# A postnorm layer on one core: the second batch's second low-rank factor later, the last norms partly on ScalarE, one queue for each half

## The chip, the cores and the metric

The kernel runs on one core of a Trainium2 chip. The metric is the time of one execution on the device in microseconds. Engines are called by the profile's names: PE (TensorE matmul), PEld (its weight load), DVE (VectorE), ACT (ScalarE), POOL (GpSimd), SP (SyncE). All data is f32.

## The reference

One transformer layer on `x` of 2 batches x 512 tokens x 512 features: grouped attention with 32 query heads and 8 key heads of size 128, then a feed-forward part with a mixture of four low-rank experts. After each part a residual is added and a layer norm without weights is applied.

```python
x = layernorm(x + attention(x) @ Wo + bo)                       # causal softmax, rotary embedding
y = x @ W_base.T + b_base                                       # 512 -> 512
z = x @ A[e].T                                                  # 4 experts, rank 8: 32 numbers a token
alpha = softmax(log(prior + eps) + (x @ router_W.T + router_b)) # over the 4 active experts
out = layernorm(x + y + sum_e alpha[e] * 2 * z[e] @ Bm[e].T)
```

## The kernel before, in words

Tokens are cut into eight tiles of 128: four (`TPB`) of the first batch, four of the second. Attention is a software pipeline over the tiles of all head groups, driven by `slot(T)`. At its end the feed-forward part starts, one object `Ffn` a tile. Nothing is rearranged by a scheduler: each engine executes its instructions in the order in which the Python code issues them, and the code after the last `slot` is an order written out by hand.

The steps of one `Ffn`, which the code calls as methods:

- `stats`, `centre`, `transpose`: the first norm (with `norm1.root` for the reciprocal root of the variance), and the tile transposed by PE.
- `base(c)`, c = 0 to 3: two matmuls for each quarter of the features, one into each of the tile's two PSUM banks `py[0]` and `py[1]`. Each bank holds 256 of the 512 outputs, and beside them half of `z`; the second holds the router's four logits too (L679). In the profile each matmul appears as two records, so that `base` of all four quarters is "x16".
- `logits`, `alphas`: DVE adds the prior and takes the maximum (L696, L698), ACT takes the exponential (L705), DVE normalises (L706, L707) and multiplies `z` by the weights into `zs` (L710).
- `low_rank`: PE transposes `zs` into the PSUM tile `tz` (L719), and DVE copies that to `zT` (L720). `tz` lies in the pool `ps_k`, which has one buffer, so that two tiles' `low_rank` share it.
- `finish`: the second low-rank factor, two matmuls of 33 rows that add onto `py` (L724, "x4").
- `add`: DVE adds the residual from both banks into `y` (L730) and takes the second norm's statistics (L634, L635).
- `norm2.root` (ACT square root L638, DVE reciprocal L639), then `store`: POOL subtracts the mean and multiplies (L642), SP's queue sends the tile out (L754).

The last tile is done differently. `route` computes its `z` and logits ahead by matmuls of 16 and 20 columns (L689). `half` and `half_end` compute 256 outputs at a time and add the residual and the low-rank part in PSUM (L738, L744, L745); `half_stats` takes the statistics from there (L748, L750); `store_halves` normalises each half out of PSUM (L642) and sends it (L760).

Names at the end: `fz` is the fourth tile of the first batch, `fa[0]` and `fa[1]` are the first two of the second batch in the order of work, `fb` and `fc` the last two. `fz` and `fb` use the banks `qx` and `qy`, `fa[0]` and `fc` the two `sc` banks, `fa[1]` the banks `wx` and `wy`.

The order written out by hand around the change, with the methods' names:

```python
fc.route(*CTX); fc.logits(); fc.alphas(); fa[1].logits(); fa[1].alphas()
fa[0].finish(); fa[0].add()
fa[1].low_rank()
# fb.base(0), fb.base(1), fa[1].finish(), fa[1].add(), fb.base(2), fb.base(3)
fc.low_rank()
# roots and stores of fz and fa; fb.logits, fb.alphas; first half of fc; fb.low_rank
# second half of fc with fb.finish and fb.add inside; fb's root and store; fc's
```

Of the kernel before, what the change touches and what calls it, by code (L numbers as in the profile page):

```python
# [9 lines left out]
F32 = mybir.dt.float32  # L10
I32 = mybir.dt.int32
AF = mybir.ActivationFunctionType
ALU = mybir.AluOpType
AX = mybir.AxisListType

P = 128
# [13 lines left out]
def postln_layer_kernel(  # L30
# [33 lines left out]
    nc = tc.nc  # L64
# [35 lines left out]
    outf = out.flatten_outer_dims()  # L100
# [17 lines left out]
    OH, ARH = O // 2, EAR // 2  # L118
# [54 lines left out]
    for n in range(2):  # L173
# [6 lines left out]
        out=tri, in_=tri, pattern=[[-BLK, QB], [-1, BLK]], compare_op=ALU.is_ge,  # L180
# [221 lines left out]
    halves = {}  # L402
# [221 lines left out]
    class Norm:  # L624
# [16 lines left out]
        def apply(self, i, dst, src=None, engine=nc.vector):  # L641
            engine.tensor_scalar(  # L642
                dst, dst if src is None else src, self.mv[:, i, 0:1], self.rstd[:, i : i + 1], ALU.subtract, ALU.mult)

    class Ffn:


# [101 lines left out]
            if n:  # L749
                nc.vector.bn_aggr(self.norm2.mv[:, self.i, :], self.st)  # L750

        def store(self):
            self.norm2.apply(self.i, self.y, engine=nc.gpsimd)
            nc.sync.dma_start(out=outf[ts(self.t, P), :], in_=self.y)  # L754

        def store_halves(self):
            for n, queue in enumerate((nc.sync, nc.scalar)):
                cols = ts(n, OH)
                self.norm2.apply(self.i, self.y[:, cols], self.py[n])
                queue.dma_start(out=outf[ts(self.t, P), cols], in_=self.y[:, cols])  # L760


    NP = len(parts)
# [209 lines left out]
    def tiles(ts_, banks, name):  # L973
        n = len(ts_)
        norms = Norm(ffn_pool, n, f"a{name}"), Norm(ffn_pool, n, f"f{name}")
        return [Ffn(t, bank, *norms, i) for i, (t, bank) in enumerate(zip(ts_, banks))]

    f0 = tiles(range(TPB), ((QX, QY), (QX, QY), (SC, SC), (QX, QY)), "0")
    fa = tiles([TPB + i for i in order[:2]], ((SC, SC), (WX, WY)), "1a")
# [75 lines left out]
    fa[1].alphas()  # L1055
    fa[0].finish()
    fa[0].add()
    fa[1].low_rank()
    for c in range(KC):
        fb.base(c)  # L1060
        if c == 1:
            fa[1].finish()
            fa[1].add()
    fc.low_rank()
    fz.norm2.root(3, TPB)
    fa[0].norm2.root(0, 2)
    for f in (fz, *fa):
# [12 lines left out]
            fb.add()  # L1080
    fc.half_end(1)
    fb.norm2.root(0, 1)
    fb.store()
    fc.half_stats(1)
    fc.norm2.root(0, 1)
    fc.store_halves()
# [50 lines left out]
```

## Time and profile before

| | |
|---|---|
| median of 3 runs | 840.73 us (840.07 to 843.15) |
| the profiled execution, its own time | 840.69 us |
| its span, first to last instruction | 838.9 us |
| PE busy | 826.0 us, 98% of the span |
| DVE, ACT, POOL busy | 595.7, 353.1, 292.3 us |
| mean granted PE clock | 0.996 |

The span is what the profile shows in detail; 1.8 us of the execution's own time lie around it. A row of the timeline gives start, duration, engine, line, operation, what it writes and reads, and in brackets the idle time of the engine before it with what ended that. The chain lists, from the end backwards, the work that each step had to wait for. The granted clock (PEclk) is 1.00 at full speed. Times below are microseconds from the start of the span, in the profiled execution.

### The profile page before, as it was taken

The page shows a single profiled execution, that of the slowest core. Times are in us where ns is not written, and L with a number is a line of the kernel's source. Part 1 is how long each engine was busy: PE and PEld are TensorE (multiplying, and loading weights), DVE is VectorE, ACT ScalarE, POOL GpSimd, SP SyncE. Part 2 cuts the span into 40 slices and gives each one's busy share as a digit, 9 for nine tenths or more (in the row PEclk, how much of TensorE's full clock was granted, in tenths as well). Part 3 has the DMA queues.
Part 4 walks back from the last instruction along what each step waited for, and adds up shares of the span by engine and source line. Part 5 has one row for each costly group of instructions (what it writes and reads, how often), then busy time and mean ns, then how long its engine had stood idle before and what let it go on. Part 6 is the DMA issues. An engine that isn't in the chain of part 4 may idle for free.

```text
span 838.9 us, 10734 instructions
## 1 busy us (share of the span) xinstructions
PE 826.0 (98%) x3201; PEld 583.9 (70%) x3201; DVE 595.7 (71%) x1963; ACT 353.1 (42%) x1000; POOL 292.3 (35%) x319
## 2 busy tenths in 40 slices
PE   9999999999999999999999999999999999999996
PEld 5567767677777777777777777777777776645564
DVE  5468977787767876786867867687767968853534
ACT  1225454544435344434435444434434444762132
POOL 6463344233332334233332334344323523300023
PEclk9999999999999999999999999999999999999998
DMA  9127536463653566362653566274644546574211
GB/s 287 40 64 195 151 97 183 110 181 108 156 157 99 164 162 174 77 188 88 154 149 104 163 159 182 69 217 116 153 129 133 164 110 191 165 236 113 62 39 63
DMA packets 84971, 116.47 MB, mean 139 GB/s; under 512 B 6581, under 2 KB 64797, under 8 KB 82866
## 3 DMA queue, kind: packets, MB, share of 16 engines
q1 hardware_dynamic: 84258, 115.50, 48.2%
q0 software_dynamic: 448, 0.14, 0.2%
q8 instruction: 25, 0.41, 0.2%
q14 instruction: 32, 0.26, 0.1%
q10 hardware_dynamic: 208, 0.15, 0.1%
HBM read 71.73 MB, written 44.04 MB: 138 GB/s over the span
## 4 chain that ended last, share of the span: by engine, by line
PE 92%; DVE 3%; DMA 1%; ACT 1%; POOL 1%; issue 1%; SPq 0%; DVEq 0%; POOLq 0%
PE pc L544 16%; PE sc L488 13%; PE qx L429 11%; PE wx L429 11%; PE pp L355 10%; PE qy L429 8%; PE wy L429 8%; PE pv L342 7%; PE py L679 3%; PE po L615 3%; PE tp L274 1%; PE py L724 1%; DMA x_sb<-_attn_hidden_states_dram 1%; DMA pT<-db 0%; DVE wt L568 0%
## 5 line engine op out<-in xcount | busy, mean ns | idle before, releaser
L503 ACT ACTIVATE p<-sc,nmax 128x288 f32<-128x288 f32 (+15 forms) x256 | 124.5, 486 | 253.0 <-DVE nmax L496 207.5
L496 DVE CUSTOM_DVE_ANT_0 sc<-sc,maskw 128x288 f32<-128x288 f32 (+15 forms) x256 | 114.2, 446 | 154.4 <-PE sc L488 151.7
L544 PE MATMUL pc<-pT,v 128*128 128x512 f32 x320 | 165.5, 599 | 0.5 <-DMA pT<-db 0.5
L488 PE MATMUL sc<-kT,qT 128*128 128x160 f32 (+15 forms) x512 | 162.0, 398 | 1.2 <-ACT p L503 1.1
L376 POOL TENSOR_TENSOR qT<-q,t 128x512 f32<-128x512 f32 x56 | 71.1, 1269 | 188.0 <-DVE q L375 188.0
L511 ACT ACTIVATE p<-p,den 128x288 f32<-128x288 f32 (+15 forms) x256 | 133.5, 522 | 0.1
L488 PEld LDWEIGHTS sc<-kT,qT 128*128 128x128 f32 x512 | 96.7, 190 | 30.3 <-issue 14.3
L416 POOL TENSOR_TENSOR cs<-ctxT 128x256 f32<-128x256 f32 x28 | 26.5, 947 | 196.1 <-PE wy L429 109.5
L550 ACT COPY ctxT<-pc 128x512 f32<-128x512 f32 x64 | 37.5, 586 | 124.0 <-PE pc L544 124.0
L519 DVE STREAM_TRANSPOSE zt<-p 128x128 f32<-128x128 f32 (+2 forms) x192 | 81.6, 425 | 0.0
L544 PEld LDWEIGHTS pc<-pT,v 128*128 128x128 f32 x320 | 57.0, 190 | 19.5 <-issue 5.7
L355 PE MATMUL pp<-xT,wk 128*128 128x512 f32 x128 | 65.0, 593 | 0.5 <-ACT xT L275 0.5
L342 PE MATMUL pv<-wv,xT 128*128 128x256 f32 x256 | 63.6, 379 | 0.0
L429 PE MATMUL wx<-wo,ctxT 128*128 128x256 f32 x224 | 57.7, 380 | 0.4 <-DVE den L507 0.4
L429 PE MATMUL qx<-xs,wq 128*128 128x256 f32 x224 | 58.0, 381 | 0.0
L342 PEld LDWEIGHTS pv<-wv,xT 128*128 128x128 f32 x256 | 48.5, 190 | 13.4 <-issue 6.9
L521 DVE STREAM_TRANSPOSE zt<-p 128x32 f32<-128x32 f32 (+3 forms) x256 | 57.4, 224 | 0.0
L429 PEld LDWEIGHTS qx<-xs,wq 128*128 128x128 f32 x224 | 41.4, 190 | 22.3 <-issue 16.0
L429 PEld LDWEIGHTS wx<-wo,ctxT 128*128 128x128 f32 x224 | 42.4, 190 | 13.5 <-issue 7.7
L503 ACT ACTIVATION_READ_ACCUMULATOR p<-sc,nmax 128x1 f32 x256 | 49.9, 195 | 0.0
L601 DVE TENSOR_TENSOR x_sb<-wx,x_sb 128x256 f32<-128x256 f32 x112 | 46.9, 419 | 0.0
L368 DVE SCALAR_TENSOR_TENSOR t<-q,bqkT,rope_sb 64x512 f32<-64x512 f32 x56 | 43.0, 768 | 1.3
(187 smaller groups left out, 1364.3 us busy)
## 6 DMA issues: line engine op xcount, KB each, us to landing
db<-zt SPq DMA_DIRECT2D x64, 256.0 KB, 4.3
pT<-db SPq DMA_DIRECT2D x16, 1024.0 KB, 4.8
db<-zt SPq DMA_DIRECT2D x64, 192.0 KB, 3.3
pT<-db SPq DMA_DIRECT2D x16, 768.0 KB, 4.4
wq<-in_L_attn_Wq_dram SPq DMA_DIRECT2D x20, 512.0 KB, 4.7
wo<-in_L_attn_Wo_dram SPq DMA_DIRECT2D x10, 1024.0 KB, 7.5
db<-zt SPq DMA_DIRECT2D x64, 128.0 KB, 2.4
pT<-db SPq DMA_DIRECT2D x16, 512.0 KB, 4.1
```

What stands on the lines that cost most here:

```text
L342: nc.tensor.matmul(psq["v", gg, t], lhsT=xT[:, c, ts(t, P)], rhs=wvs[gg][0][:, c, :], start=(c == 0), stop=(c == KC - 1))
L355: nc.tensor.matmul(psq[key], lhsT=wt[:, c, cols], rhs=xT[:, c, ts(b, S)], start=(c == 0), stop=(c == KC - 1))
L376: nc.gpsimd.tensor_tensor(dst, t1[:].rearrange("p (n s) -> p n s", s=BLK), t2[:].rearrange("p (n s) -> p n s", s=BLK), ALU.add)
L429: nc.tensor.matmul(ps, lhsT=wt[:, c, :], rhs=xt[:, c, :], start=start and c == 0, stop=c == CH - 1, skip_group_check=True)
L488: nc.tensor.matmul(sc[s][:, :w], lhsT=qT[u][:, i * QB + n].rearrange("p r s -> p (r s)"), rhs=kT[u][:].rearrange("p n s -> p (n s)")[:, :w ...
L496: nc.vector.tensor_tensor_reduce(sc[s][:, :w], sc[s][:, :w], maskw[:, S - w :], -SCALE, -MASKED, ALU.add, ALU.min, nmax[s])
L503: nc.scalar.activation(ptile[s][:, :w], sc[s][:, :w], AF.Exp, bias=nmax[s], scale=-1.0, accum_out=rden[s])
L511: nc.scalar.activation(ptile[s][:, :w], ptile[s][:, :w], AF.Copy, scale=rden[s])
L519: nc.vector.transpose(z[:, :, last - i : last, n, :].rearrange("p q j s -> p j q s"), ptile[s][:, : i * P])
L521: nc.vector.transpose(z[:, : n + 1, last, n, :], ptile[s][:, i * P : w])
L544: nc.tensor.matmul(psc[p], lhsT=v_sb[g // VG, b * TPB + j][:, ts(g % VG, D)], rhs=pT[p][:, :, ts(j, P)], start=(j == 0), stop=(j == i))
L601: nc.vector.tensor_tensor(into, pw[k, bank], into, ALU.add)
```

## The change

It does three things. `fa[1].low_rank` moves from before `fb.base(0)` to after `fb.base(2)`, and `fa[1].finish` and `fa[1].add` move from after `fb.base(1)` to after `fc.low_rank`. The second norm of `fb` is applied by ACT instead of POOL, as `rstd * y + shift` with a `shift = -mean * rstd` computed by one more DVE instruction; the first half of `fc` is treated in the same way, and its second half stays on DVE. The two halves of `fc` swap queues: the first goes out by ACT's queue, the second by SP's.

```diff
+        def apply_act(self, i, dst, src=None):
+
+            shift = self.pool.tile([P, 1], F32, tag="shift", name="shift", bufs=2)
+            mean, rstd = self.mv[:, i, 0:1], self.rstd[:, i : i + 1]
+            nc.vector.scalar_tensor_tensor(shift, mean, -1.0, rstd, ALU.mult, ALU.mult)
+            nc.scalar.activation(dst, dst if src is None else src, AF.Identity, bias=shift, scale=rstd)
...
-        def store(self):
-            self.norm2.apply(self.i, self.y, engine=nc.gpsimd)
+        def store(self, on_act=False):
+            if on_act:
+                self.norm2.apply_act(self.i, self.y)
+            else:
+                self.norm2.apply(self.i, self.y, engine=nc.gpsimd)
             nc.sync.dma_start(out=outf[ts(self.t, P), :], in_=self.y)
 
         def store_halves(self):
-            for n, queue in enumerate((nc.sync, nc.scalar)):
-                cols = ts(n, OH)
-                self.norm2.apply(self.i, self.y[:, cols], self.py[n])
-                queue.dma_start(out=outf[ts(self.t, P), cols], in_=self.y[:, cols])
+
+            halves = [self.y[:, ts(n, OH)] for n in range(2)]
+            self.norm2.apply_act(self.i, halves[0], self.py[0])
+            self.norm2.apply(self.i, halves[1], self.py[1])
+            for n, queue in enumerate((nc.scalar, nc.sync)):
+                queue.dma_start(out=outf[ts(self.t, P), ts(n, OH)], in_=halves[n])
...
     fa[0].finish()
     fa[0].add()
-    fa[1].low_rank()
     for c in range(KC):
         fb.base(c)
-        if c == 1:
-            fa[1].finish()
-            fa[1].add()
+        if c == 2:
+            fa[1].low_rank()
     fc.low_rank()
+    fa[1].finish()
+    fa[1].add()
     fz.norm2.root(3, TPB)
     fa[0].norm2.root(0, 2)
...
-    fb.store()
+    fb.store(on_act=True)
     fc.half_stats(1)
```

## The prediction

> **What bounds the kernel now.** I read the page first, for the engine that carries the chain, then the chain over the last 24 us, then the granted clock in half microseconds around the one long wait on it, and last the timeline of ACT, POOL and the queues at the end.
>
> ```profile
> span 838.9 us, 10734 instructions
> PE 92%; DVE 3%; DMA 1%; ACT 1%; POOL 1%; issue 1%; SPq 0%; DVEq 0%; POOLq 0%
> ```
>
> PE carries the chain nearly everywhere. All edits lie after 817 us, so only PE's idle time and the tail behind its last matmul can be won. The chain over that stretch (start, length, what):
>
> ```profile
> 818.97 0.27 DVE zs L710 x2
> 819.24 0.04 issue
> 819.28 0.40 PE tz L719
> 819.68 3.11 PE py L679 x8
> 822.79 1.06 PE py L724 x4
> 823.84 2.04 PE py L679 x8
> 825.89 0.11 PE tz L719
> 826.00 1.73 PE ph L738 x8
> ```
>
> `fa[0].finish` ends at 817.28; then PE waits for `fa[1]`'s `zs`, its longest wait of the whole trace (2.0 us). The first half of `fb.base` then takes 3.11 us for 8 records; at the rate of other `base` stretches (16 records in 3.69 us) they would take 1.85. The clock says why (columns: window, length, PE, PEld, DVE, ACT, POOL busy, granted clock, DMA):
>
> ```profile
> 818.00:818.50 0.50, 0.00 (x0) 0.00 (x0) 0.05 (x1) 0.40 (x3) 0.00 (x0) 1.00 0.00 0
> 818.50:819.00 0.50, 0.00 (x0) 0.00 (x0) 0.42 (x3) 0.50 (x1) 0.00 (x0) 0.69 0.00 0
> 819.00:819.50 0.50, 0.22 (x2) 0.22 (x3) 0.50 (x4) 0.50 (x1) 0.00 (x0) 0.50 0.00 0
> ...
> 822.00:822.50 0.50, 0.50 (x3) 0.28 (x2) 0.00 (x0) 0.00 (x0) 0.00 (x0) 0.90 0.00 0
> ```
>
> The clock falls to 0.50 at about 818.7, after 1.4 us of waiting, and comes back at about 822.1: 3.4 us at half speed. The wait costs 2.0 us, 0.3 in the transpose and 1.26 in the slow matmuls.
>
> Further on, the softmax of `fb` hangs on ACT:
>
> ```profile
> 825.29 0.29 ACT L638 ACTIVATE rstd_f1a<-mv_f1a,eps_sb 128x2 f32<-128x2 f32 x1 [5.21 <-DVE mv_f1a L635]
> 825.60 1.28 ACT L705 ACT_TABLE_LOAD   x1
> 826.89 0.30 ACT L705 ACTIVATE al<-lg,nmx 128x4 f32<-128x4 f32 x1
> ```
>
> The root of `fa[1]`'s norm stands ahead of `fb`'s exponential on ACT, with a table load between. So `fb`'s `zs` comes a fixed time after `fa[1].finish`: that ends at 823.84, `zs` at 828.04, 4.2 us later. Here nobody waits for it, since PE has work until 828.78. At the end:
>
> ```profile
> 832.96 2.08 POOL L642 TENSOR_SCALAR y<-y,mv_f1b,rstd_f1b 128x512 f32<-128x512 f32 x1 [0.28 <-DVE rstd_f1b L639]
> 834.78 0.54 DVE L642 TENSOR_SCALAR y<-ph,mv_f1c,rstd_f1c 128x256 f32<-128x256 f32 x1
> 835.06 0.33 SPq L754 DMA_DIRECT2D out_dram<-y  x1
> 835.35 0.41 ACTq L760 DMA_DIRECT2D out_dram<-y  x1
> 835.49 0.38 SPq L760 DMA_DIRECT2D out_dram<-y  x1
> ```
>
> `fc`'s first half is ready at 834.86, but SP's queue sends it at 835.49, behind `fb`'s store, which waited for POOL. Three transfers (512 KB) then travel together.
>
> **Part 1, the order on PE.** Nothing is removed or added; one transpose and two matmuls move on PE, with their copy and additions on DVE. They issue no DMA and pass none. After `fa[0].finish` (chain end 817.29) PE goes on: three quarters of `fb.base`, 12 records at 0.231 = 2.77, to 820.06; `fa[1]`'s transpose (0.11; its `zs` is there since 819.24) to 820.17; the last quarter, 0.92, to 821.09. `fc`'s transpose needs the single `tz` buffer, free when DVE has copied `fa[1]`'s: that copy stays behind `fa[0].add` on DVE, where it is now (820.75 to 821.00), so at most 0.1 is lost; I take 0.05. Then 0.11 for the transpose and 1.06 for `fa[1].finish`: it ends at 822.3 instead of 823.84, 1.5 earlier. On DVE `fc`'s copy is now ahead of `fa[1].add`; it ends near 821.7, before the addition's data (821.9), and costs nothing. With a slow `finish` it would still hide.
>
> The cover of `fb`'s softmax is gone, however. Between `fa[1].finish` and `fb`'s transpose PE keeps only the first half of `fc`: 1.73 + 0.43 + 0.63 = 2.79. `zs` still needs 4.2: addition 0.85, statistics 0.69 and 0.18, root 0.29, table load 1.28, exponential, reciprocal and two products 1.1, less 0.2 of overlaps (the first addition starts 0.4 before `finish` ends, the rest are gaps between engines). PE would wait 822.3 + 4.2 + 0.04 - (822.3 + 2.79) = 1.45 us. `fb`'s transpose starts at 826.55 instead of 828.78: **2.2 us earlier**. Queued behind it are `fc`'s second half and `fb.finish`. Behind `zs` on DVE stand `fc`'s first statistics (0.43) and `fb`'s copy (0.26), to 827.2; `fb.finish` needs it at 827.6. No further wait. The three POOL norms and their SP stores move with the roots and end near 830.5, before `fb`'s.
>
> **The clock in the new wait.** The trace has one precedent: fallen after 1.4 us of waiting. The Trainium skill, page "TensorE: Matmul & The Clock Gate", section "Part 1: The HAM clock gate", says instead that the clock halves after a whole idle window of about 3.4 us that runs free of the kernel. The 3.4 us of slow clock fit such a window, its condition doesn't: the window before the fall held 1.1 us of `finish` and `route`'s narrow matmuls. By the page the new wait costs its 1.45 alone; by the precedent it adds half of 3.41, 1.7 us. I take no fall, since 1.7 us and more of wide matmuls stand ahead of this wait, where `route`'s 16 and 20 columns stood before the old one. From below: a phase without a fall was possible in the runs before too, so nothing is gained beyond the 1.26 counted.
>
> **Part 2, the tail,** in times of before (all 2.2 earlier later). `shift` is one small DVE instruction: 0.16 (a 128x1 reciprocal) to 0.23 (the 128x4 product); I take 0.18. Identity with two per-row operands isn't in the trace: the Copy with one took 0.726 for 128x512 and 0.511 for 128x256, the exponential from PSUM 0.474 for 128x256 against 0.366 for a copy without one, so an operand is worth 0.11. Bounds 0.73 to 0.84 and 0.47 to 0.62; I take 0.82 and 0.57.
>
> `fb`: reciprocal to 832.85, shift to 833.07, ACT to 833.92, SP issues at 833.95 instead of 835.06. POOL's 2.08 go. `fc`'s statistics are ready at 833.08, just as the shift ends. `fc`'s root wants ACT at 833.79 and finds it busy until 833.92: 0 to 0.15 late, I take 0.1. Then reciprocal to 834.38, shift to 834.60, DVE's half to 835.16 (SP issues 835.19), ACT's half to 835.20 (ACT's queue issues 835.23, nothing behind it). The last issue was 835.49: 0.26 won. Landing took 2.3 us with three transfers in flight and 2.0 for a 256 KB store alone: 0.3 more. Tail **0.55**, bounds 0.1 and 0.9.
>
> One rule speaks against ScalarE here: "ScalarE: Activation LUTs", section "Rules for kernel authors", gives additions and products to VectorE. The rows agree on the halves (0.54 on DVE, 0.57 plus a shift on ACT): splitting them ends only 0.1 before two in a row on DVE (835.31). For `fb` the rule would cost more: 0.55 on DVE (L642, 128x512) would stand ahead of `fc`'s statistics, and the sum would be about 0.5 worse; on ACT it lies beside DVE's work.
>
> **Sum:** 2.2 + 0.55 = 2.75. The profiled execution took 840.69 (span 838.9 and 1.8 around it); the median, 840.73, is the same. 840.69 - 2.75 = 837.94, so 837.9 us, 0.33% less.
>
> **Rivals.**
> *The clock falls again* in the new wait, or already behind `route`: +1.6, 839.5 us. For: the precedent at 818.7. Against: wide matmuls ahead of it.
> *Identity brings table loads* (slower). Place: ACT between the roots of `fb` and `fc`, and behind the latter. A load is 1.28. `fb`'s Identity starts 0.9 late, the root of `fc` then waits for it and a second load, 2.3 late in all, and a third load ahead of the half adds 0.85: +3.15, 841.1 us. It decides from 2.75 on, so only if both kinds of reload occur. Against: the Copy of the trace ran between exponentials with no load, and the skill's page on activations, section "Table sets", counts identity among the fillers of every set.
> *The wait is only moved:* `fc`'s transpose finds `tz` taken or `fb`'s softmax is later still, and PE gives all 2.2 back; the tail alone is left: 840.1 us. Against: the copy at 820.75.
> *No new wait:* `zs` comes in time and 1.45 more is won, 836.5 us. It would need the table load to be hidden, which the order on ACT excludes.
>
> **How the numbers follow.** Forecast 0.62, clock 0.25, loads 0.05, moved 0.05, no wait 0.03. The forecast's own terms leave 837.0 to 838.8. The range takes in the clock rival with its own spread, and on the low side a landing at its better bound: 836.4 to 840.6. About 0.5% (4.2 us: 836.5 and 844.9) is what a measurement can tell from no change. Faster: a tenth of the forecast (a better landing, a smaller wait) and the last rival, 0.09. Slower needs 7 us more than forecast, twice any price above: 0.03, for what no row shows. Same 0.88.
>
> **What would show it.** Right: no idle PE before `fa[1]`'s transpose and full clock around 819; about 1.4 us of idle PE before `fb`'s, waiting for DVE `zs`; Identity of 0.8 us with no table load near it; last issue at about 833.0, last PE record at about 830.9. Wrong: a clock of 0.5 after 826, table loads at the new ACT line, or a wait for `tz` at 821.

## The result, and the profile after

| | before | changed |
|---|---|---|
| median, measured together (22 runs each) | 842.83 us | 838.87 us |
| lowest and highest | 839.87, 846.49 | 836.55, 841.85 |
| ratio, 95% interval | | 0.9960 (0.9948 to 0.9971) |
| measured together once more (50 and 22 runs) | 841.32 us | 838.39 us |
| ratio, 95% interval | | 0.9967 (0.9954 to 0.9979) |
| the profiled execution, its span | 840.69, 838.9 us | 839.75, 838.0 us |

The change makes the kernel 0.3 to 0.4% faster. The forecast was 0.33%, but the two profiled executions are only 0.94 us apart where it said 2.75. Where that went is seen in the profile after. First the page's span and chain by engine: PE still carries it.

```profile
span 838.0 us, 10735 instructions
PE 90%; DVE 4%; DMA 2%; ACT 1%; issue 1%; POOL 1%; SPq 0%; DVEq 0%; POOLq 0%
```

The chain of waits behind `route` (start, length, what):

```profile
814.77 1.70 PE zl L696 x16
816.47 1.06 PE py L731 x4
817.53 4.65 PE py L686 x12
822.18 0.11 PE tz L726
822.29 0.93 PE py L686 x4
823.22 0.11 PE tz L726
...
828.32 0.27 DVE zs L717 x2
828.58 0.04 issue
828.62 0.29 PE tz L726
```

The old wait is gone: `fb.base` (L686, 12 records) starts the moment `fa[0].finish` (L731) ends, and `fc`'s transpose at 823.22 follows without a wait for `tz`. But the 12 records take 4.65 us, not 2.77. The granted clock is the last but two of the columns (window, length, PE, PEld, DVE, ACT, POOL, clock, DMA share, GB/s):

```profile
816.00:817.00 1.00, 1.00 (x8) 0.91 (x8) 0.32 (x2) 0.10 (x1) 0.00 (x0) 1.00 0.00 0
817.00:817.50 0.50, 0.50 (x4) 0.17 (x2) 0.17 (x1) 0.28 (x2) 0.00 (x0) 1.00 0.00 0
817.50:818.00 0.50, 0.50 (x2) 0.44 (x2) 0.45 (x4) 0.00 (x0) 0.00 (x0) 0.51 0.00 0
...
820.50:821.00 0.50, 0.50 (x3) 0.38 (x2) 0.47 (x2) 0.00 (x0) 0.00 (x0) 0.58 0.00 0
```

The clock falls at 817.5 and returns at 820.9, although PE has no idle moment in these rows. The 3.4 us ahead of the fall held 1.70 us of `route`'s matmuls of 16 and 20 columns, 1.0 us of `finish`, whose matmuls have 33 rows, and 0.6 us of `base`.

The new wait is where it was forecast, and behind ACT's table load. PE's waits, and ACT's timeline there:

```profile
PE tz L726 <- DVE zs L717: 1.3, 1, 1.3
```

```profile
825.82 0.29 ACT L638 ACTIVATE rstd_f1a<-mv_f1a,eps_sb 128x2 f32<-128x2 f32 x1 [5.50 <-DVE rstd_f L639]
826.14 1.28 ACT L712 ACT_TABLE_LOAD   x1
827.43 0.30 ACT L712 ACTIVATE al<-lg,nmx 128x4 f32<-128x4 f32 x1
```

The tail, from the timeline of ACT, DVE and the queues:

```profile
833.00 0.81 ACT L650 ACTIVATE y<-y,shift,rstd_f1b 128x512 f32<-128x512 f32 x1 [0.43 <-DVE shift L649]
833.72 0.28 ACT L638 ACTIVATE rstd_f1c<-mv_f1c,eps_sb 128x1 f32<-128x1 f32 x1
834.30 0.54 DVE L642 TENSOR_SCALAR y<-ph,mv_f1c,rstd_f1c 128x256 f32<-128x256 f32 x1
834.42 0.56 ACT L650 ACTIVATE y<-ph,shift,rstd_f1c 128x256 f32<-128x256 f32 x1 [0.42 <-DVE shift L649]
834.87 0.33 SPq L772 DMA_DIRECT2D out_dram<-y  x1
835.01 0.38 ACTq L772 DMA_DIRECT2D out_dram<-y  x1
```

Identity runs with no table load right ahead of it, `fc`'s root starts 0.05 after its statistics end (833.67), and both halves are sent within 0.14 us of each other.

Two stretches can be measured in every profile, apart from where in the pipeline they begin: the PE stretch from the end of `fa[0].finish` to the end of the last matmul, and the end stretch from there to the end of the span. Before: 817.28 to 833.05 and on to 838.9, so 15.77 + 5.85. Changed: 817.53 to 832.95 and on to 838.0, so 15.42 + 5.05. The end gave 0.8 us, PE only 0.35 (and the stretch began 0.25 later).

### The profile page after: what moved, and what is told of

Its sections match the earlier page's. It is cut to its first block, busy times and chain, and to the rows that moved or that the text cites. A ratio compares the mean times of both kernels' runs of the same rounds, so it can differ in the third digit from the quotient of the medians.

```text
span 838.0 us, 10735 instructions
## 1 busy us (share of the span) xinstructions
PE 825.9 (99%) x3201; PEld 583.9 (70%) x3201; DVE 595.6 (71%) x1964; ACT 354.3 (42%) x1002; POOL 290.1 (35%) x318
## 4 chain that ended last, share of the span: by engine, by line
PE 90%; DVE 4%; DMA 2%; ACT 1%; issue 1%; POOL 1%; SPq 0%; DVEq 0%; POOLq 0%
PE pc L544 16%; PE sc L488 13%; PE qx L429 11%; PE wx L429 11%; PE pp L355 9%; PE qy L429 8%; PE wy L429 8%; PE pv L342 6%; PE py L686 3%; PE po L615 3%; DMA pT<-db 1%; PE tp L274 1%; PE py L731 1%; DMA db<-zt 1%; DMA x_sb<-_attn_hidden_states_dram 1%
```

## The experiments

Theory: the order takes about 2 us out of the PE stretch, and the clock's fall, which no longer needs a wait of PE, takes 1.7 of it back in the profiled execution; the tail gains 0.8. Rivals: the order only moves the wait; the tail's gain belongs to another of its parts; the clock is lowered by waiting alone, or by something else.

One fall of 3.41 us at half speed lowers the mean clock of an execution by 0.5 x 3.41 / 840 = 0.0020. The clock after the last matmul is in the mean too, so that an execution without a fall reads 0.997 to 1.0; 0.998 or more is taken here as no fall, 0.996 or less as at least one, 0.995 or less as at least two; 0.997 is left undecided by it.

**Each half of the change alone.** `order_only` is the changed kernel with the last norms and queues as before:

```diff
-    fb.store(on_act=True)
+    fb.store()
```

(and `store_halves` as before).

> The new order on PE alone; the last norms and the queues stay as before. Theory (the order is worth 2.2 us where the clock stays up, and about 0.4 where it falls behind route, as in the profile of the changed kernel; the tail is worth about 0.8): 0.8 us slower than the changed kernel, 1 to 2.5 us faster than before, with the wait of 1.3 to 1.5 us ahead of fb's transpose. Rival (the order only moves the wait, and the gain is the tail's): within 0.3 us of before.

`tail_only` keeps the order of before and takes the new norms and queues.

> The last norms on ACT and the swapped queues alone; the order on PE as before. Theory: fb's store leaves about 1.1 us earlier, the last issue 0.4 us and the end 0.8 us earlier than before, so 0.5 to 1.0 us faster than before. Rival (the tail gains nothing, since ACT then starts fc's root late): within 0.2 us of before, fc's root 0.15 us late or more.

Measured: `order_only` 839.62 us against 841.56, ratio 0.9966 (0.9955 to 0.9978), 1.9 us between the medians; the wait ahead of `fb`'s transpose is 1.3 us. Its PE stretch is 818.27 to 833.70, 15.43 with a fall of the clock, and its end stretch 5.9 us, so that in these profiles neither part disturbs the other. Its ratio is no worse than the changed kernel's (0.9960 and 0.9967), though 0.8 us more was expected: a difference of that size is within the intervals. `tail_only` is 840.57, ratio 0.9987 (0.9966 to 1.0008): the 1.0 us of its median is not clear of noise, but its end stretch is 833.99 to 839.0, 5.0 us, as in the changed kernel, with `fc`'s root 0.05 late and not 0.15. So the order does not just move the wait; and the tail gains, which only the end stretches of the profiles show, not the whole times.

`tail_only` shows what the order had to deal with. Its chain and clock around the old wait:

```profile
819.38 0.39 PE tz L726
819.78 3.65 PE py L686 x8
823.43 1.36 PE py L731 x4
```

```profile
817.00:817.50 0.50, 0.46 (x2) 0.00 (x0) 0.29 (x2) 0.14 (x2) 0.00 (x0) 0.67 0.00 0
817.50:818.00 0.50, 0.00 (x0) 0.00 (x0) 0.43 (x5) 0.00 (x0) 0.00 (x0) 0.50 0.00 0
...
824.00:824.50 0.50, 0.50 (x4) 0.35 (x2) 0.11 (x1) 0.00 (x0) 0.00 (x0) 1.00 0.00 0
```

Here the clock falls at about 817.2, while `finish` still runs and before the wait begins, and stays low until 824.0, twice 3.41 us; the wait fills most of the first half of that. The 8 records of `fb.base` cost 1.8 us more than the 1.85 of full speed, and `fa[1].finish` 0.3 more. This is the price of the old order that the profile of before, with one fall, does not show. In the 67 executions of before measured beside these kernels, 36 have a mean clock of 0.995 or less (28 of them 0.994 or less) and none 0.998 or more. Of 22 of the changed kernel none has 0.995 or less, and 11 have 0.998 or more.

**What lets the clock fall.** `after_wide` widens `route` in the changed kernel (its tile `zl` grows with it, which is left out here):

```diff
-                        zl[:, n, :w], lhsT=self.xT[:, c, :], rhs=wbT[:, c, n, OH : OH + w],
+                        zl[:, n, :], lhsT=self.xT[:, c, :], rhs=wbT[:, c, n, w : OH + w],
```

> The changed kernel with route's 16 and 20 column matmuls replaced by as many of 256 columns, of which the last 16 or 20 are used; this adds 1.9 us of PE work on its path. Theory (what lets the clock fall is a window filled with narrow matmuls, with or without a wait): no fall of the clock between 810 and 828 in the profile, a mean clock of 0.998 or more in every run, and no more than 0.7 us slower than the changed kernel on average, since half of its executions or more no longer lose 1.7 us. Rival (the wide matmuls are no different, what counts is waiting or total load): the clock falls as often as in the changed kernel, and it is 1.9 us slower.

`before_wide` is the same edit in the kernel before:

> The kernel before with route's matmuls widened to 256 columns (1.8 us more PE work); the wait of 2.0 us for fa[1]'s zs stays. Theory A (narrow matmuls and waits count alike as idle): the old wait alone still lets the clock fall in some executions, but mean clocks of 0.992 and below, two falls in a row, become rare (under 1 in 10; 28 of 67 executions of before had 0.994 or less). Theory B (only the wait counts): as many falls as before and 1.8 us slower than it. Theory C (only narrow matmuls count): no fall in any execution, and 0 to 1 us slower than before or faster.

In the profile of `after_wide` there is no fall. Its chain:

```profile
814.28 3.46 PE zl L696 x16
817.74 1.06 PE py L731 x4
818.79 2.97 PE py L686 x12
```

The same 12 records take 2.97 us instead of 4.65, and the PE stretch is 818.79 to 832.54, 13.75 us against 15.42. That is the changed kernel's stretch without a fall, 2.0 us below before's; the fall costs 1.67. The whole kernel is 839.83 us (ratio 0.9982, 0.9967 to 0.9997) in spite of 1.76 us more in `route`. But the expectation of no fall in any execution failed: 9 of 22 have 0.997 or less, which is no clear difference from the 11 and 12 of 22 of the changed kernel, at a median of 841.98 against 839.45 of the other 13. Nor did it stay within 0.7 us of the changed kernel: by the ratios it is 1.3 to 1.9 us slower, so that the whole times hardly show a gain from it. Narrow matmuls are not the only cause, and the 2.5 us between the two groups are more than the 1.67 of one fall. The wait of 1.3 us, which this kernel still has, is the next suspect.

`before_wide`, with the wait of 2.0 us and no narrow matmuls, took 841.98 us, ratio 1.0007 (0.9992 to 1.0021), so that 1.8 us of added work cost about 0.6 (at most 1.8 by the interval). Of its 14 executions 5 have 0.998 or more, where before has none, and the lowest mean is 0.993; 3 have 0.995 or less. Theory C fails, since without narrow matmuls 8 of 14 still have 0.996 or less; theory B fails on the 5, and only just on the time; theory A's "under 1 in 10" holds for 0.992 and below (none of 14, against 10 of 50 of before), though 14 executions are few.

`roots_wide` and `roots_late` take the new wait away as well. Both move this, and let ACT normalise `fa[1]` (abridged):

```diff
     fc.low_rank(); fa[1].finish(); fa[1].add()
-    fz.norm2.root(3, TPB); fa[0].norm2.root(0, 2); (stores of fz, fa)
     fb.logits(); fb.alphas()
     ...
     fb.low_rank()
+    fz.norm2.root(3, TPB); fa[0].norm2.root(0, 2); (stores of fz, fa; fa[1] on_act=True)
```

> The changed kernel with the roots and stores of fz and fa moved from ahead of fb's logits to behind fb's low_rank, and fa[1]'s norm applied by ACT so that POOL has two norms and not three. Theory (the new wait of 1.3 us ahead of fb's transpose is the root and the table load that stand ahead of fb's exponential on ACT): the wait falls to 0.2 us or less, and the kernel is about 1.2 us faster than the changed one. Rival (the wait is fb's own softmax on DVE, or POOL's norms become the end): a wait of 0.8 us or more stays, or the last issue is a store of fa behind POOL, and the time is within 0.4 us of the changed kernel.

> Both suspects of the clock taken away: the kernel with roots and stores behind fb's low_rank (no wait of PE there), and route's matmuls 256 columns wide (1.8 us more PE work). Theory (9 of 22 executions of the changed kernel with wide matmuls alone still lost clock, in the wait ahead of fb's transpose; 11 of 22 with the wait alone gone lost it behind route): with both gone hardly any execution loses it, mean clock 0.998 or more in 20 of 22 or more, and the highest time within 2 us of the lowest. Rival (something else lowers the clock): 8 or more of 22 with 0.997 or less.

`roots_late` has no wait left. Its chain around `fb`'s transpose:

```profile
823.42 0.43 PE ph L751 x2
823.86 0.63 PE ph L752 x2
824.48 0.22 PE tz L726
824.70 0.87 PE ph L745 x4
```

Its PE stretch is 816.33 to 828.74, 12.4 us, 1.3 below `after_wide`'s: the new wait was indeed the roots and the table load that stood ahead of the exponential on ACT. Yet the median is 838.61 (ratio 0.9964, 0.9951 to 0.9977), no faster than the changed kernel. The end stretch has grown from 5.05 to 834.9 - 828.74 = 6.2 us: POOL ends `fa[0]`'s norm only at 829.6, and on SP's queue the stores of `fa[1]` and `fb` wait behind its store, so that three stores leave just ahead of the halves, which then take 2.7 and 2.6 us to land instead of 1.7 and 1.9:

```profile
829.64 1.30 SPq L764 DMA_DIRECT2D out_dram<-y  x3
831.04 0.39 SPq L772 DMA_DIRECT2D out_dram<-y  x1
```

And `route` is still narrow: 11 of 22 have 0.997 or less, at 839.04 against 837.47 of the others.

`roots_wide` (839.17, ratio 0.9977, 0.9965 to 0.9989) shows two groups: 15 executions of 838.4 to 839.9 us, and 6 of 841.7 to 843.0 with 0.996 or 0.997. By the mean clock 10 of 21 have 0.997 or less (4 of them in the faster group), where the rival had said 8 or more: the expectation failed, and the rival, that something else lowers the clock, was met. The 6 slow executions are some 3 us behind the others, again more than one fall. A cause of long executions other than narrow matmuls and the two waits remains; what and where it is, is not known, since no profiled execution caught it.

`after_again` is the changed kernel once more:

> The changed kernel itself once more, beside the others on one chip. Expected: 0.3 to 0.45% faster than before, a fall of the clock behind route in about half of the executions (11 of 22 had a mean clock of 0.997 or less), and those about 1.5 us slower than the others.

It repeats the result (0.9967) and the halves: 12 of 22 with 0.997 or less, at 839.3, and 10 with more, at 837.4. Four have 0.995 or less, which the first measurement had not shown.

What makes the difference within one kernel can be read from `all_dve`, a kernel of the next part, which differs from the changed one only in its last norms. On PE it is the same code, `route` narrow, yet in its profile the clock does not fall there:

```profile
814.95 1.70 PE zl L696 x16
816.64 1.06 PE py L731 x4
817.70 2.97 PE py L686 x12
```

Its PE stretch is 817.70 to 831.45, again 13.75 us. In every profile the clock also falls in the tail, where PE is idle. In the changed kernel that is at 834.57, 17.06 us or five times 3.41 after the fall at 817.51; the other profiles with both falls have 17.06 or 17.07 (`tail_only` six times 3.41). So the falls lie on a grid of 3.41 us. First the row of the changed kernel, then that of `all_dve`:

```profile
834.50:834.60 0.10, 0.00 (x0) 0.00 (x0) 0.10 (x1) 0.10 (x1) 0.00 (x0) 0.86 0.00 0
833.60:833.70 0.10, 0.00 (x0) 0.00 (x0) 0.10 (x1) 0.00 (x0) 0.00 (x0) 0.78 0.00 0
```

Counted back five steps from 833.66, `all_dve` has a boundary at 816.6, just between `route` and `finish`: the step with `route` also held 1.7 us of `base`. In the changed kernel `route` and `finish` lay in one step with only 0.6 us of `base`. Around `route`, the steps ahead of a fall held 0.8 us or less of `base` in all profiles with a fall, and those without a fall 1.3 us or more of `base` or of widened `route`. This fits a clock that follows the amount of wide matmuls in each step; it is read from some ten profiles, and no run separates the share of `finish`, nor explains the long executions of `roots_wide`.

**Which part of the tail.** Three kernels were profiled once each: `queues_only` (before, with `enumerate((nc.scalar, nc.sync))`), `fb_act_only` (before, with `fb.store(on_act=True)`) and `all_dve` (the changed kernel, with `self.norm2.apply` on DVE in place of `apply_act` in both places).

> The kernel before with nothing but the queues of the two halves swapped. From PE's last matmul to the last issue it was 2.44 us before, with the first half's transfer held on SP behind fb's store. Theory (SP waits for POOL's norm either way): the second half is issued on SP at the same place, ACT's queue sends the first 0.5 us earlier; last issue the same within 0.1 us, end within 0.3 us. Rival (the swap is the gain): 2.1 us and the end 0.5 us nearer.

> The kernel before with nothing but fb's last norm on ACT. Theory (this is most of the tail's gain): fb's store is issued 1.1 us earlier, the first half no longer waits on SP, the last issue is the second half on ACT's queue, 2.35 us after PE's last matmul, and the end comes 0.5 us or more nearer to PE's last matmul (5.85 us before, 5.05 in the changed kernel). Rival (the halves make the gain): 5.6 us or more from PE's last matmul to the end.

> The changed kernel with all last norms on DVE (fb's and both halves of fc's), the queues as changed. Theory: fb's norm of 0.55 us stands ahead of fc's second statistics on DVE, so these start 0.3 to 0.5 us later; from PE's last matmul to the last issue 2.6 to 3.0 us instead of 2.06. Rival (one shift less and one engine change less make up for it): 2.2 us or less.

Queue issues of `queues_only`, then of `fb_act_only`:

```profile
834.56 0.38 ACTq L760 DMA_DIRECT2D out_dram<-y  x1
835.16 0.38 SPq L760 DMA_DIRECT2D out_dram<-y  x1
```

```profile
834.49 0.33 SPq L771 DMA_DIRECT2D out_dram<-y  x1
834.95 0.38 ACTq L771 DMA_DIRECT2D out_dram<-y  x1
```

| from the last matmul's end | last issue | end of the span |
|---|---|---|
| before (833.05) | 2.44 | 5.85 |
| `queues_only` (832.72) | 2.44 | 5.7 |
| `fb_act_only` (832.65) | 2.30 | 5.15 |
| `all_dve` (831.45) | 2.55 | 5.35 |
| changed (832.95) | 2.06 | 5.05 |

`fb`'s norm on ACT is 0.7 of the 0.8 us: its store is under way before the halves are. The swapped queues alone leave the last issue where it was. Splitting the halves, with the queues swapped, brings the last issue 0.24 nearer and the end 0.1. With all three on DVE about half of the later issue comes from the order of two instructions, the rest from the two halves in a row:

```profile
831.29 0.55 DVE L642 TENSOR_SCALAR y<-y,mv_f1b,rstd_f1b 128x512 f32<-128x512 f32 x1
831.75 0.42 DVE L755 BATCH_NORM_STATS2 st<-ph 128x6 f32<-128x256 f32 x1
832.45 0.29 ACT L638 ACTIVATE rstd_f1c<-mv_f1c,eps_sb 128x1 f32<-128x1 f32 x1 [1.40 <-DVE mv_f1c L757]
832.98 0.99 DVE L642 TENSOR_SCALAR y<-ph,mv_f1c,rstd_f1c 128x256 f32<-128x256 f32 x2
```

`fc`'s statistics could have started at about 831.5 and stand behind `fb`'s norm, so that `fc`'s root comes 1.00 after the last matmul instead of 0.77. From the root to the end of the halves it is 1.52 instead of 1.26. The last issue is 0.5 later than in the changed kernel, just under the range that was expected; of that 0.3 reaches the end.

**A version without both causes.** `best` alternates `route` and `fb.base`, one matmul of each in turn, with `fa[0].finish`, `fa[1].low_rank` and `fa[1].finish` among them; `fa[1]`'s softmax comes ahead of `fc`'s, and the roots of `fz` and `fa` behind `fb.low_rank`; ACT normalises `fz` and `fa[1]`, POOL `fa[0]`, whose store now stands last of the three on SP. `best2` only moves three calls forward:

```diff
     for k in range(2 * KC):
         fc.route_step(k // KC, k % KC)
         fb.base_step(k // 2, k % 2)
         if k == 1: fa[0].finish(); fa[0].add()
-        elif k == 4: fa[1].low_rank()
-        elif k == 6: fa[1].finish(); fa[1].add()
+        elif k == 2: fa[1].low_rank()
+        elif k == 4: fa[1].finish(); fa[1].add()
     fc.logits(); fc.alphas(); fb.logits()
```

> The changed kernel with a new order at the end: route's narrow matmuls alternate with fb's base matmuls, fa[1]'s softmax stands ahead of fc's, the roots and stores of fz and fa come behind fb's low_rank, and fz and fa[1] are normalised by ACT, fa[0] by POOL. Theory (the clock falls where a window of 3.4 us holds narrow matmuls or a wait; the new wait is the root and table load on ACT): no wait of PE over 0.3 us after 810, mean clock 0.998 or more in at least 20 of 22 executions, about 3 us faster than the changed kernel in the median, 4 to 6 us faster than before. Rival (the falls come from elsewhere, the load of the whole stage or the pipeline before it): falls in a third of the executions or more, and no more than 1.5 us faster than the changed kernel.

> The new order once more, with fa[1]'s low_rank, finish and add two steps earlier among the alternating matmuls, so that DVE has done fa[1].add before the route matmuls end. In the first version fc's logits stood 1.1 us behind fa[1].add on DVE, and PE waited 0.7 us for fc's zs. Theory: that wait goes, 0.7 to 1.1 us faster than the first version (836.0 to 836.5 us), no fall of the clock. Rival (PE's wait is replaced by fb's softmax, or DVE is the bound of the stage): within 0.3 us of the first version.

`best`: 837.11 us (6 runs), ratio 0.9944 (0.9925 to 0.9964). `best2`: 836.18 us (8 runs), ratio 0.9941 (0.9919 to 0.9963). None of the 14 executions has a mean clock below 0.998. In `best` PE waited 0.7 us for `fc`'s `zs`, since `fc`'s logits stood behind `fa[1].add` on DVE; the expectation of no wait over 0.3 and of 3 us against the changed kernel failed with that (about 1.3 in the medians). In `best2` the wait is gone; the chain shows what the alternation costs:

```profile
820.25 0.56 PE py L702 x2
820.81 0.13 PE zl L696 x2
820.94 0.55 PE py L702 x2
821.49 0.13 PE zl L696 x2
```

A pair of narrow records takes 0.13 instead of 0.21, the pair of `base` behind it 0.55 instead of 0.46, so the alternation saves no work of PE; in these 14 executions it kept the clock up. Which of the changes made together in `best` does that is not separated. `best2` beats before by 0.6%. Its advantage of 2 us over the changed kernel is read from medians of few runs in separate measurements, whose intervals against before still touch. One of its 8 executions took 840.75 us at a mean of 0.998, so long executions without a fall exist too, and are not explained.

## Why the prediction was right, and where it was not

The forecast was 837.9 us, 2.75 below before. Against before measured beside it, the changed kernel gained 3.96 us in the first measurement and 2.93 in the second.

- *The old wait goes, `tz` isn't in the way, the rest of DVE hides.* Right: no wait between `finish` and 827.3 in the profile, and `fc`'s transpose at once after the last quarter of `fb.base`.
- *`zs` of `fb` comes 4.2 us after `fa[1].finish`, PE waits 1.45.* Right: 4.2 and 1.26 (1.3 in the waits). `roots_late` shows its cause by removing it.
- *2.2 us on PE.* Right where the clock holds: 15.77 to 13.75, 2.0 us (`all_dve` and `after_wide`). In the profiled execution 0.35.
- *The clock: "I take no fall".* This step failed, in half of the executions. The forecast gave the fall a quarter of the chance and 839.5 us; the profiled execution took 839.75. It weighed the wrong place: its reason was the wide matmuls ahead of the new wait, while the fall came 10 us earlier behind `route`, with PE busy throughout, which the rival named in half a sentence. The Trainium skill's page "TensorE: Matmul & The Clock Gate", section "Part 1: The HAM clock gate", asks for a whole idle window; the rows at 817.5 show a fall without any idle time, so the measurement decides. The length of 3.4 us agrees, and so does the free run of the window: the two falls of that trace lie five times 3.41 us apart.
- *Nothing is gained beyond the 1.26 of one fall.* Also wrong, and in the other direction: before loses two windows or more in about half of its executions (36 of 67), the changed kernel rarely (0 of 22 and 4 of 22). An estimate from these counts, at 1.7 us a window: before lost 0.9 us or more on average that was not counted, the changed kernel 0.85. That these two errors nearly cancel is luck, and the number came out right with its help.
- *Tail 0.55.* Right in mechanism, measured 0.8. Two terms were too small: the last issue is 0.38 earlier after PE's last matmul, not 0.26, and the landing behind it 0.4 shorter, not 0.3. The costs of Identity were right (0.81 and 0.56 against 0.82 and 0.57), the delay of `fc`'s root smaller (0.05 against 0.1). For DVE in place of ACT, weighed with the Trainium skill's page "ScalarE: Activation LUTs", section "Rules for kernel authors", the forecast said about 0.5 worse for `fb` and 0.1 for the halves. `all_dve` issues 0.5 later in all, 0.23 from `fb` and 0.26 from the halves, and ends 0.3 later: ACT was the better engine, but the two terms were mis-sized.
- *No table load for Identity.* Right: none near L650.

## What to carry to other kernels

A gap on PE should be judged with the granted clock of the windows around it, and over several executions: one profile shows one phase of the clock, and the same code lost no, one or two windows of 3.4 us here. When a wait is filled, look for the instruction whose distance is fixed by another engine (here a root and a table load ahead of an exponential): it sets the next wait. A last norm belongs where nothing of the last tile queues behind it, and its store where it no longer shares the end with other stores.

## What the runs showed of the hardware that was not expected

The clock fell to half with PE busy in every row of the profile: at 817.5 in the changed kernel, for 3.4 us, behind 1.7 us of matmuls of 16 and 20 columns and 1.0 us of matmuls of 33 rows. With the former widened to 256 columns, and a boundary of the grid at nearly the same place (817.47, counted back from the fall at 834.53 in the tail), 12 records behind them took 2.97 us instead of 4.65 in the profiled executions, at the price of 1.76 us more in `route`. Over the executions the effect is not clear: a mean clock of 0.998 or more in 13 of 22, against 11 (and 10) of 22. The same narrow matmuls cost nothing where the grid lay otherwise (`all_dve`). Where the wait of 1.9 us fell into a slow step, the clock stayed low for 6.8 us (`tail_only`).
